# A 16-block fp32 transformer step: elementwise pairs of the norms moved to GpSimd, one demodulation kept in its PSUM bank, block 0's key demodulation by one-hot products, and new instruction orders

## The chip, the cores and the metric

One core of a Trainium2 chip. The core has TensorE (PE) for matmuls, VectorE (DVE), ScalarE (ACT) and GpSimd (POOL) for elementwise work, and SyncE (SP), which issues most transfers; each takes its instructions in the order of its own queue. The metric is the device time of one execution in microseconds, the median over the runs.

## The reference

A batch of 128 sequences of 64 tokens with 256 features, `x` (8192 tokens in all), goes through four residual layers, each conditioned on vectors of the sequence:

```python
x = x + L0(x, cond_512)   # kx = demodulated linear of x * style_k; softmax(kx kx^T / 4) kx, 16 heads of 16;
                          # then a demodulated linear with style_o
x = x + L1(x, cond_512)   # relu(x @ w_down[b]) @ w_up[b] + x, weights made per sequence
x = x + L2(x, ids, ...)   # h = ln(ln(x) * pw_g[id] + pw_b[id]) ...; t, s: ln(x) with table gains;
                          # m, n, r: x plus a vector of the sequence;
                          # silu([h t m n r s] @ W1 + b1) @ W2 + b2, then ln
x = x + L3(x, cond_512)   # out = x @ (U[b] V) + bias[b], U from cond_512 @ W_dec, rank 30
```

`demodulated` means that output column o of sequence b is multiplied by rsqrt(sum_i (w[o,i] * style[b,i])^2 + 1e-8). Everything is fp32 apart from one-hot tables in bf16.

## The kernel before

The tokens are cut into NBLK = 16 blocks of T = 512 tokens (NB = 8 sequences); a block has NTILE = 4 tiles of 128 tokens. `attention(blk)` makes layer 0 of a block, `rest(blk, ...)` layers 1 to 3. A prologue (`prologue_keys`, `prologue_rest`) makes styles, demodulations, tables, the sequence vectors, and the decoder factors U of all sequences.

Layouts alternate: features on partitions (`xT`, `x1T`, `x2T`, `xnT`, `hnT`, `g`; 128 x 2 x 512) for the wide matmuls, tokens on partitions (`x2`, `xn`, `h`, `x3`; four 128 x 256) for norms. TensorE's transposes lead from one to the other.

In a block: `xsT` = xT * style on GpSimd (L840). For each of the four tiles (`tile_attention`): keys (L930); `kxe` = bank * demodulation `dmk` on VectorE (L938); plus bias on GpSimd (L944); a 32 x 32 transpose on VectorE (L955); scores into the four banks `sc` (L986); their row maxima `mt` on VectorE (L995, two of 128x1024 per tile); the maxima are transposed (L1005, L1011, L1018, L1025) and subtracted by one-hot products (L1036); exp on ScalarE (L1050); the weighted sum (L1060); normalization (L1072 to L1079); a transpose (L1090) and the output style (L1095). Then the output linear (L896), for each half of the features:

```python
y = bank * demod_o                  # L903, VectorE, PSUM -> SBUF slot "tmp"
x1T = y + ob + xT                   # L914, VectorE
```

Layer 1 is L1118 (down), L1127 (relu), L1136 (up) and the sum x2T = 2 * x1T + up (L1149, VectorE, two halves). Layer 2 transposes x2T (L1190), copies it (L1193), takes statistics (L408, L409 on VectorE), r = (var + eps)^-0.5 on GpSimd (`rstd`, L413 and L415), the offset nr = -mean * r on VectorE (`offset`, L1168), and normalizes on ScalarE (`normalize`, L1176). `h` = xn * gain (L1201, VectorE) + shift (L1208, GpSimd), with gain and shift gathered per token (`pw`, L855), is normalized again. `xnT` and `hnT` come by transposes (L1226) and copies (L1229), are multiplied by gains made with one-hot products (L1235, L1244), and go into the first linear (L1259, 16 matmuls of 512 columns with L1268). L1274 and L1277 make the silu, L1290 the second linear, L1295 its bias; the third norm follows, then x3 = normalized * lg (L1301, VectorE) + x2 (L1304, GpSimd). Layer 3 transposes x3 (L1316, L1321), multiplies by U of the block (`uT`, L1333), adds a bias (L1344), multiplies by V (L1359), adds x3 (L1367) and stores (L1371).

For `dmk` the prologue writes the demodulations of all sequences to DRAM (`demod_k`, L505), and every block reads its eight rows back, each repeated over 64 partitions (two transfers, L797). U goes to DRAM through `uu` (128 x 4096): for each of the two halves of the features 30 products (L750), the bias (L755), and four transfers to `ud` (L769); both halves use the same `uu`.

The order of the work is not that of the program text. `Plan` records every operation with its engine, an assumed duration, what it reads and writes and the buffer slots it needs, then walks through an assumed execution and, on each engine, takes among the operations that could start first the one with the lowest turn. The turns are tables of numbers, `TURNS`: one for the prologue, one for the first block, one for all middle blocks, one for the last. `KEEP` favours a matmul of the tiling mode that TensorE is in; `pair=True` marks a VectorE operation that in the plan shuts GpSimd out; `load` gives a transfer's assumed time. Slots are handed out in the same walk, and some pass to heirs (`HEIRS_*`) once the prologue is done with them.

Of the kernel before, what the change touches and what calls it, by code (L numbers as in the profile page):

```python
# [9 lines left out]
F32 = mybir.dt.float32  # L10
# [3 lines left out]
ALU = mybir.AluOpType  # L14
AX = mybir.AxisListType

B, S, F = 128, 64, 256
NT = B * S
C = 2
T = 512  # L20
NB = T // S
NBLK = NT // T
NTILE = T // 128
H, D = 16, 16
K3 = 30
K3P = 32
# [6 lines left out]
SLOTS_FT = (("xT", 2), ("xsT", 1), ("osT", 1), ("x1T", 2), ("x2T", 2), ("hnT", 1), ("xnT", 1), ("g", 1), ("s2", 1))  # L33
SLOTS_1 = (("att", 2), ("p1", 8))
SLOTS_2 = (("kT", 2), ("kR", 2), ("v", 1), ("ao", 2), ("tmp", 3), ("pw", 3), ("p2", 8))
SLOTS_U = 16

HEIRS_1 = ("x3", "x2", "h", "xn", "x3", "x2", "h", "x3")
HEIRS_U = ("x2", "x2", "x2", "x2", "xn", "xn", "xn", "xn", "h", "h", "h", "h", "x3", "x3", "x3", "x3")
HEIRS_2 = ("pw", "v", "kT", "kR", "pw", "tmp", "ao", "v")  # L40
# [17 lines left out]
class Plan:  # L58
# [10 lines left out]
    SWITCH, KEEP = 0.08, 30.0  # L69
# [7 lines left out]
    def op(self, eng, took, emit, reads=(), writes=(), busy=None, claims=(), full=0.0, mode=0, pair=False):  # L77
# [3 lines left out]
        o = dict(eng=eng, took=took, busy=took if busy is None else busy, emit=emit, full=full, mode=mode, pair=pair)  # L81
# [34 lines left out]
    def order(self):  # L116
# [18 lines left out]
        at, self.cells, landed, mode, locked = {}, {}, [], 0, 0.0  # L135
        ready = [o for o in ops if not o["wait"]]
        done = []
        while ready:
            best = {}
            for o in ready:  # L140
                pe = o["eng"] == "PE"
                other = at.get("POOL", 0.0) if o["pair"] else locked if o["eng"] == "POOL" else 0.0
                t = max([other, at.get(o["eng"], 0.0)] + [ops[d]["end"] + lag for d in o["deps"]])
# [8 lines left out]
                if t is not None:  # L152
                    turn = o["prio"] - (self.KEEP if pe and o["mode"] == mode else 0.0)
                    best.setdefault(o["eng"], []).append((t, turn, o["n"]))
# [16 lines left out]
            o["start"], o["end"] = t, t + busy + (o["took"] - o["busy"])  # L171
# [26 lines left out]
    -8200 -7966 -18394 1443 -1847 8122 14127 3541 20535 -16013 -17005 17606 -23774 5435 -34510 18558 2614 3537 -253  # L198
    20624 27103 -438 -1494 25293 9034 -42362 -12205 -43231 28467 -41057 -40764 10345 1927 -10856 23480 5587 -11535
    -2699 -12811 11563 -1709 -22299 -17435 24238 -9733 103 2193 12913 3946 2640 -12255 -6755 -6353 2747 30512 7567  # L200
    -13172 -40570 9903 5897 -16559 -43835 2104 4978 -9021 8382 5714 28619 2514 -41088 -38702 21169 -15013 -4235 -6370
    -36126 27882 -7087 5065 6270 7617 -15738 -41818 -24576 -46135 -5769 -179 25293 -47598 501 -36248 -39392 -5815
    -17772 -6386 -44534 12570 -44284 -21576 -10573 -19779 6641 3353 -10423 -12878 -41598 -36305 18779 -11277 5632
# [1291 lines left out]
```

## Time and profile before

| | |
|---|---|
| median of 3 runs (lowest, highest) | 927.48 us (926.0, 928.22) |
| the profiled execution: time, span | 929.13 us, 927.4 us |
| mean granted TensorE clock | 0.972 |
| busy: TensorE, VectorE, GpSimd, ScalarE | 826.4, 698.2, 509.8, 446.5 us |
| HBM read, written | 75.94 MB, 13.24 MB |

The span reaches from the first to the last instruction; the time has a little around it. A row of a group of instructions gives line, engine, operation, what it writes and reads, how many, busy time and mean duration, and then the engine's idle time before them with what ended it. A wait reads "engine line <- engine line": who waited for whom. A window gives each engine's busy time in a stretch, and in parentheses how many instructions. Neighbouring instructions of one engine overlap by some hundredths of a microsecond in the records.

### The profile page before, as it was taken

The numbers are of one execution on the slowest core, as the hardware profiler recorded it, in microseconds if no ns is written. First come the engines' busy times: TensorE is split into PE (matmuls) and PEld (weight loads), VectorE is DVE, ScalarE is ACT, GpSimd is POOL, SyncE is SP. The second block draws the span as 40 slices with busy tenths as digits, with TensorE's granted clock in tenths as the row PEclk, the third lists the DMA queues.
The fourth block names the chain that finished last, engine by engine and source line by source line (L and its number), as shares of the span: only waits on it lengthen the run. The fifth ranks groups of instructions, "written<-read, shape, count | busy, mean of one in ns | idle before, by whom it ended". The sixth has DMA issues, their size and how long they took to land.

```text
span 927.4 us, 23950 instructions
## 1 busy us (share of the span) xinstructions
PE 826.4 (89%) x9744; PEld 535.9 (58%) x9744; DVE 698.2 (75%) x1539; ACT 446.5 (48%) x821; POOL 509.8 (55%) x602
## 2 busy tenths in 40 slices
PE   3686889898999999998989999999989899899893
PEld 2465646556565656666565656566665656465542
DVE  3595976969696987969696969879696969686643
ACT  1452444537364554545373645545453736444331
POOL 4371771837557482838475573829384755724221
PEclk9697999999999999999999999999999999999896
DMA  8866641232415132332324152322323231202000
GB/s 258 226 175 212 198 131 56 82 101 82 124 47 149 56 115 69 98 93 82 112 82 124 47 149 56 108 74 92 101 80 113 76 98 48 80 3 58 12 24 24
DMA packets 63103, 90.75 MB, mean 98 GB/s; under 512 B 6352, under 2 KB 46736, under 8 KB 62992
## 3 DMA queue, kind: packets, MB, share of 16 engines
q1 hardware_dynamic: 57872, 72.43, 26.9%
q0 software_dynamic: 5120, 16.78, 6.3%
q8 instruction: 77, 1.26, 0.6%
q14 instruction: 34, 0.28, 0.1%
HBM read 75.94 MB, written 13.24 MB: 96 GB/s over the span
## 4 chain that ended last, share of the span: by engine, by line
PE 71%; DVE 17%; DMA 3%; ACT 3%; issue 2%; POOL 1%; SPq 0%; another core or an unknown queue 0%; DVEq 0%; POOLq 0%; ACTq 0%
PE bank L1259 24%; PE sc L986 7%; PE bank L1060 7%; PE bank L1290 6%; PE bank L896 6%; DVE mt L995 5%; PE bank L930 4%; PE bank L973 3%; DVE x2T L1149 2%; PE bank L1190 2%; PE bank L1118 2%; PE bank L1226 2%; PE sc L1036 1%; PE bank L1090 1%; DVE st L408 1%
## 5 line engine op out<-in xcount | busy, mean ns | idle before, releaser
L995 DVE TENSOR_REDUCE mt<-sc 128x8 f32<-128x1024 f32 x128 | 154.6, 1211 | 11.8 <-PE sc L986 8.2
L1050 ACT ACTIVATE e<-sc 128x1024 f32<-128x1024 f32 x128 | 126.5, 1030 | 64.7 <-PE sc L1036 56.4
L1005 ACT COPY mt<-mt 128x16 f32<-128x16 f32 x64 | 13.0, 203 | 165.0 <-DVE mt L995 164.8
L1079 POOL TENSOR_TENSOR att<-ao,rz 128x256 f32<-128x256 f32 x44 | 27.2, 623 | 100.0 <-DVE rz L1076 92.5
L930 PE MATMUL bank<-wk,xsT 128*128 128x256 f32 x256 | 68.4, 402 | 0.4 <-ACT p L976 0.4
L1244 DVE TENSOR_TENSOR hnT<-hnT,bank 128x512 f32<-128x512 f32 x32 | 21.9, 688 | 59.8 <-PE bank L1235 39.2
L1259 PE MATMUL bank<-g,w_t 128*128 128x512 f32 x128 | 63.2, 617 | 4.1 <-DVE g L1244 4.1
L1259 PE MATMUL bank<-hnT,w_h 128*128 128x512 f32 x128 | 63.9, 605 | 1.4 <-DVE hnT L1244 1.4
L1259 PE MATMUL bank<-xnT,w_s 128*128 128x512 f32 x128 | 65.1, 593 | 0.0
L1290 PE MATMUL bank<-w,s 128*128 128x256 f32 x256 | 62.5, 386 | 0.7 <-DVE s L1277 0.7
L896 PE MATMUL bank<-osT,wo 128*128 128x512 f32 x128 | 60.9, 602 | 0.6 <-DVE osT L1095 0.6
L1259 PE MATMUL bank<-x2T,w_x 128*128 128x512 f32 x128 | 60.8, 595 | 0.0
L413 POOL TENSOR_SCALAR ry<-mvy 128x4 f32<-128x4 f32 (+1 forms) x19 | 9.2, 482 | 91.9 <-DVE mvy L409 91.7
L944 POOL TENSOR_TENSOR kxe<-kxe,kbr 128x256 f32<-128x256 f32 x64 | 46.8, 732 | 22.5 <-DVE kxe L938 18.0
L986 PEld LDWEIGHTS sc<-kR,kT 24*128 24x128 f32 x1408 | 44.1, 189 | 24.0 <-issue 12.5
L986 PE MATMUL sc<-kR,kT 24*128 24x128 f32 x1408 | 52.5, 286 | 3.4 <-ACT e L1050 3.4
L930 PEld LDWEIGHTS bank<-wk,xsT 128*128 128x128 f32 x256 | 47.6, 201 | 9.9 <-issue 3.7
L1290 PEld LDWEIGHTS bank<-w,s 128*128 128x128 f32 x256 | 46.0, 190 | 9.1 <-DVE s L1277 2.2
L408 DVE BATCH_NORM_STATS2 st<-uu 128x6 f32<-128x256 f32 x118 | 47.4, 409 | 2.1 <-ACT uu L1193 1.4
L870 POOL TENSOR_TENSOR wdn<-gdb,late 128x512 f32<-128x512 f32 x32 | 40.8, 1277 | 10.0 <-PE bank L1118 5.3
L855 POOL DMA_INDIRECT pw<-in_pw,idx x39 | 38.7, 993 | 11.5 <-issue 8.9
L1060 PE MATMUL bank<-e,p 128*32 128x128 f32 x1280 | 44.9, 276 | 0.0
(193 smaller groups left out, 2064.1 us busy)
## 6 DMA issues: line engine op xcount, KB each, us to landing
xT<-in_xT SPq DMA_DIRECT2D x32, 256.0 KB
dmk<-demod_k SPq DMA_DIRECT2D x32, 256.0 KB
gdb<-dgdb SPq DMA_DIRECT2D x16, 512.0 KB
ubb<-ugub SPq DMA_DIRECT2D x32, 256.0 KB
wup<-ugub SPq DMA_DIRECT2D x32, 256.0 KB
out_x<-uu SPq DMA_DIRECT2D x37, 128.0 KB
ud<-uu SPq DMA_DIRECT2D x8, 512.0 KB
uT<-ud SPq DMA_DIRECT2D x16, 256.0 KB
```

The lines of the kernel that those rows point to most:

```text
L408: dve(256, lambda: nc.vector.bn_stats(st.t, x.t), [x], [st])
L855: lambda tl=tl, n=n: nc.gpsimd.indirect_dma_start(out=pw[tl].t, out_offset=None, in_=a["pw"], in_offset=bass.IndirectOffsetOnAxis(ap=idx[: ...
L870: lambda w=w, dp=dp: nc.gpsimd.tensor_tensor(w(), gdb.t[:, :, 0:64], dp, ALU.mult),
L896: nc.tensor.matmul(ps.t, owT[:, c, bass.ts(oc, 128)], osT.t[:, c, :], start=(c == 0), stop=(c == C - 1))
L930: nc.tensor.matmul(ps.t[:, :F], xsT.t[:, c, bass.ts(tl, 128)], kwT[:, c, :], start=(c == 0), stop=(c == C - 1))
L944: lambda: nc.gpsimd.tensor_tensor(kxe.t[:, :, 0:D], kxe.t[:, :, 0:D], heads(kinds["kbr"][0]), ALU.add),
L986: nc.tensor.matmul(sc.t[:, q, bass.ts(g, 128)], of_g(kT.t)[r, g, :], of_g(kR.t)[r, g, :], start=(g == 0), stop=(g == 3))
L995: lambda two=two: nc.vector.tensor_reduce(mt.t[:, two, 0:4], sc.t[:, two, :].rearrange("p q (g n) -> p q g n", g=4), AX.X, ALU.max),
L1050: lambda k=k: nc.scalar.activation(es[k].t, sc.t[:, 2 * k : 2 * k + 2, :], AF.Exp, scale=0.25),
L1060: nc.tensor.matmul(ps_o.t[32 * q : 32 * q + 32, bass.ts(g, 128)], v.t.rearrange("p (g q d) -> p g q d", g=4, q=4)[:, g, q, :], es[q // 2]. ...
L1259: lambda ps=ps, w=w, src=src, fc=fc, c=c, n=n: nc.tensor.matmul(ps.t, w.t[:, c, bass.ts(fc, 128)], src.t[:, c, :], start=(n == 0 and c == ...
L1290: nc.tensor.matmul(ps.t[:, :F], s2.t[:, c, bass.ts(tl, 128)], w2.t[:, c, :], start=(c == 0), stop=(c == C - 1))
```

## The change

- `offset`: nr = -mean * r in two GpSimd operations (the mean times -1, then times r) in place of one on VectorE, for the three norms of a block.
- h = xn * gain and x3 = normalized * lg: the multiplications move from VectorE to GpSimd, ahead of the sums that were there.
- x1T: the product with `demod_o` is written back to the PSUM bank it came from, not to a `tmp` slot; the second operation reads the bank.
- Block 0's `dmk` is made in the prologue: for each tile a product of a one-hot matrix (8 sequences x 512 tokens, a new input `seqs`) with the first eight rows of the demodulations, and a ScalarE copy. Block 0's two transfers fall away.
- U's second half gets its own `uu` (a twin); when the prologue is done with it its memory serves as `hnT`, `xnT`, `g` and `s2`, which have no slots of their own any more.
- `Plan`: transfers share one assumed queue of bytes, `KEEP` is 20 and distinguishes only tiled from untiled matmuls, and the walk has slightly different rules. No operation is marked `pair`. There are new tables for the second block and the last but one, and all numbers in the tables are new, so that the instructions on every engine, SP's transfers included, stand in another order. In that order `early` is SP's eighth transfer (it was the third).

```diff
...
-SLOTS_FT = (("xT", 2), ("xsT", 1), ("osT", 1), ("x1T", 2), ("x2T", 2), ("hnT", 1), ("xnT", 1), ("g", 1), ("s2", 1))
+SLOTS_FT = (("xT", 2), ("xsT", 1), ("osT", 1), ("x1T", 2), ("x2T", 2))
...
-SLOTS_U = 16
+SLOTS_U = 16, 4
...
+HEIRS_V = ("hnT", "xnT", "g", "s2")
...
-    SWITCH, KEEP = 0.08, 30.0
+    SWITCH, KEEP = 0.08, 20.0
...
-                    turn = o["prio"] - (self.KEEP if pe and o["mode"] == mode else 0.0)
+                    turn = o["prio"] - (self.KEEP if pe and bool(o["mode"]) == bool(mode) else 0.0)
...
-    uu = slots.tile([128, B * K3P], F32, name="uu", tag="uu")
-    kinds["uu"] = [uu[:, bass.ts(n, F)] for n in range(SLOTS_U)]
+    uus = [slots.tile([128, B * K3P], F32, name=f"uu{c}", tag=f"uu{c}") for c in range(C)]
+    for name, t, n in zip(("uu", "uv"), uus, SLOTS_U):
+        kinds[name] = [t[:, bass.ts(i, B * K3P // n)] for i in range(n)]
...
-        name = "prologue" if blk < 0 else "first" if blk == 0 else "last" if blk == nblk - 1 else "middle"
+        ends = {-1: "prologue", 0: "first", 1: "second", nblk - 2: "last but one", nblk - 1: "last"}
+        name = ends.get(blk, "middle")
...
+        seqs0 = Buf("p2")
+        load(NB, 2048, lambda: nc.sync.dma_start(out=seqs0.t[:NB, :], in_=a["seqs"]), [], [seqs0])
+        dmk0 = Buf("dmk")
+        for tl in range(NTILE):
+            ps = Buf("bank")
+            product(
+                0.43,
+                ps,
+                128,
+                slice(0, F),
+                lambda tl=tl: [(seqs0.t[:NB, bass.ts(tl, 128)], dk.t[:NB, :])],
+                [dk, seqs0],
+                [dmk0],
+            )
+            act(F, lambda ps=ps, tl=tl: nc.scalar.copy(dmk0.t[:, tl, :], ps.t[:, :F]), [ps], [(dmk0, tl)])
...
-        for half in range(2):
+        if not blk:
+            dmk = dmk0
+            plan.noted[blk] += 2
+        for half in range(2) if blk else ():
...
-            ps, y = Buf("bank"), Buf("tmp")
+            ps = Buf("bank")
...
-                lambda ps=ps, y=y, oc=oc: nc.vector.tensor_tensor(
-                    y.t.rearrange("p (b t) -> p b t", t=S),
+                lambda ps=ps, oc=oc: nc.vector.tensor_tensor(
+                    ps.t.rearrange("p (b t) -> p b t", t=S),
...
-                lambda y=y, oc=oc: nc.vector.scalar_tensor_tensor(
-                    x1T.t[:, oc, :], y.t, ob[:, oc : oc + 1], xT.t[:, oc, :], ALU.add, ALU.add
+                lambda ps=ps, oc=oc: nc.vector.scalar_tensor_tensor(
+                    x1T.t[:, oc, :], ps.t, ob[:, oc : oc + 1], xT.t[:, oc, :], ALU.add, ALU.add
...
-            dve(
-                4,
-                lambda: nc.vector.scalar_tensor_tensor(nr.t, mv.t[:, :, 0], -1.0, r.t, ALU.mult, ALU.mult),
-                [mv, r],
-                [nr],
-            )
+            pool(0.24, lambda: nc.gpsimd.tensor_scalar(nr.t, mv.t[:, :, 0], -1.0, None, ALU.mult), [mv], [nr])
+            pool(0.24, lambda: nc.gpsimd.tensor_tensor(nr.t, nr.t, r.t, ALU.mult), [nr, r], [nr])
...
-            dve(
-                256,
-                lambda tl=tl: nc.vector.tensor_tensor(h[tl].t, xn[tl].t, pw[tl].t[:, 0:F], ALU.mult),
+            pool(
+                0.65,
+                lambda tl=tl: nc.gpsimd.tensor_tensor(h[tl].t, xn[tl].t, pw[tl].t[:, 0:F], ALU.mult),
...
-            dve(256, lambda tl=tl: nc.vector.tensor_tensor(x3[tl].t, x3[tl].t, lg, ALU.mult), [x3[tl]], [x3[tl]], pair=True)
+            pool(0.65, lambda tl=tl: nc.gpsimd.tensor_tensor(x3[tl].t, x3[tl].t, lg, ALU.mult), [x3[tl]], [x3[tl]])
...
+    a["seqs"] = np.repeat(np.eye(NB, dtype=f32), S, axis=1)
```

## The prediction

> **What bounds the kernel now.** I read the page's totals first, then the chain that ended last, which repeats every 51.1 us: the two x2T operations (L1149) start at 267.01, 318.10, 369.18 us. From block 1's at 163.68 to block 14's at 830.80 lie 13 such periods, 667.1 us; before them stands a start of 163.7 us, behind them an end of 96.6 us. Then one period cut where its chain changes hands.
>
> ```profile
> span 927.4 us, 23950 instructions
> PE 826.4 (89%) x9744; PEld 535.9 (58%) x9744; DVE 698.2 (75%) x1539; ACT 446.5 (48%) x821; POOL 509.8 (55%) x602
> ```
>
> ```profile
> core 0: us, PE busy (x) PEld busy (x) DVE busy (x) ACT busy (x) POOL busy (x), PEclk, DMA share, GB/s
> 318.10:333.15 15.05, 12.47 (x184) 9.15 (x184) 14.66 (x38) 10.41 (x22) 13.40 (x15) 1.00 0.29 88
> 333.15:359.15 26.00, 26.00 (x217) 15.40 (x218) 17.07 (x33) 9.36 (x17) 14.47 (x18) 1.00 0.39 110
> 359.15:369.18 10.03, 9.87 (x198) 6.54 (x195) 9.29 (x23) 7.10 (x13) 3.27 (x5) 1.00 0.19 55
> sum 51.08, PE 48.33 PEld 31.09 DVE 41.02 ACT 26.87 POOL 31.14; mean PE 16.11 PEld 10.36 DVE 13.67 ACT 8.96 POOL 10.38
> ```
>
> The middle stretch (the first layer, L1259) is TensorE's alone: 26.00 of 26.00. In the other two VectorE is busy 23.95 of 25.08 us while TensorE loses time. So 75% for VectorE is an average over a stage where it has room and two where it is full. The waits of TensorE in this period:
>
> ```profile
> PE bank L1190 <- DVE x2T L1149: 0.9, 1, 0.9
> PE bank L1359 <- DVE zT L1344: 0.8, 1, 0.8
> PE bank L1011 <- DVE uu L1367: 0.6, 1, 0.6
> PE bank L1011 <- ACT mt L1005: 0.3, 1, 0.3
> PE bank L1259 <- DVE g L1244: 0.2, 1, 0.2
> ```
>
> Nearly all end on VectorE. They sum to 2.8, the same as 51.08 - 48.33 = 2.75 us of idle TensorE: the most that a period can give while its matmuls stay as they are.
>
> **Part 1: norms and h to GpSimd (16 blocks).** The moved rows, and the GpSimd row nearest to their successors (minimum/median/maximum ns):
>
> ```profile
> L1168 DVE SCALAR_TENSOR_TENSOR nr<-mv,r x16: 161/760/772, 117.0 to 882.6; 128x4 f32<-128x4 f32 x16
> L1168 DVE SCALAR_TENSOR_TENSOR nrh<-mvh,rh x16: 161/578/580, 135.4 to 893.5; 128x4 f32<-128x4 f32 x16
> L1168 DVE SCALAR_TENSOR_TENSOR nry<-mvy,ry x16: 151/153/162, 159.7 to 911.2; 128x4 f32<-128x4 f32 x16
> L1201 DVE TENSOR_TENSOR uu<-uu,p x17: 409/414/760, 126.2 to 890.1; 128x256 f32<-128x256 f32 x17
> L1208 POOL TENSOR_TENSOR p<-p,pw x14: 712/730/996, 119.3 to 884.9; 128x256 f32<-128x256 f32 x14
> ```
>
> VectorE loses, by this period's rows, three offsets (0.76 + 0.58 + 0.15 = 1.49 us), four L1201 (2 x 0.58 + 2 x 0.41 = 1.98) and four L1301 (2 x 0.58 + 2 x 0.42 = 2.00): 5.5 us of 41.0 (less where rows overlap by some 0.07). In the full stretches stand of these, by the timeline, the first offset (0.68 in the chain), L1201 twice (0.74) and L1301 once (0.75) in the first, and L1301 three times (about 1.18) in the third: 3.35 us. That is more than the 2.75 that TensorE idles, so VectorE stops being what decides there.
>
> GpSimd keeps its eight sums (L1208, L1304) and gets eight multiplications of 128x256 at 0.73 = 5.8 and six small operations, which I put at the row of L413 (128x4 with a constant, 0.23), 1.4 in all; a two-input 128x4 has no row but the power (1.04), which bounds it from above (three per block, 2.4 more at most); I take 0.23 as the simple one is nearer. 31.1 + 7.2 = 38.3 us of a period of 49: 78%, still below TensorE.
>
> Here a rule speaks against the change. The Trainium skill, "GPSIMD Engine Reference", Engine selection, sends elementwise work to VectorE because GpSimd is about twice as slow with two inputs. The rows give 730/414 = 1.76 for one operation. By the rule (2 x 0.41 = 0.83) GpSimd has 39.1 us, by the row 38.3; both fit, and the rule counts the engine's time, not which engine is full. What is queued behind it is the danger: the products and sums for h and for x3 are now one queue, 8 operations instead of 4, so each set ends about 8 x 0.70 - (0.45 + 4 x 0.73) = 2.2 us later, and with them the transposes of L1226 and L1316. A second page works for the change: "SBUF — State Buffer", Who interferes with whom, says that a VectorE operation with two SBUF inputs and a GpSimd operation that reads SBUF exclude each other. The row that bears on it is L1168: 0.76 and 0.58 for four elements where GpSimd works, 0.15 where it idles. With a lock the three offsets are worth 1.49 per block, without 0.46; I take the row. No large VectorE operation of the changed kernel reads two SBUF tensors, so the 0.75 to 1.0 tails of L1201 and L1208 should go too.
>
> The first norm's path: in the chain the offset ends 3.7 us after the statistics (L413 at 323.56, then a 1.27 us L883 in between, L415, a VectorE maximum, offset ended at 327.29). In the new queue stand only L413's successor, one offset product, the power, one kxe sum and the other offset product: 0.23 + 0.23 + 1.04 + 0.73 + 0.23 = 2.5 us. So 1.2 earlier.
>
> **Part 2: x1T in its bank.** L903 (0.69) keeps its length if a result into PSUM costs what one into SBUF does; no row has it; between -0.05 and +0.15 each. L914 (0.75) becomes a PSUM and an SBUF input: L1149's form, 0.68. Two of each per block: from -0.25 to +0.2, taken -0.1; a bank is held 0.7 us longer, which is in the range.
>
> **Part 3: new orders.** TensorE's matmuls in a block are the same. Between L1136 and the transposes that wait for x2T (0.9 us idle now, one small transpose between) the new order puts a transpose, the 16 shifts and two transposes, 0.11 + 0.34 + 0.22 by the chain, 0.56 more than before. So of 2.75 idle I expect 2.2 back: 0.34 of the 0.9 and some 0.2 elsewhere stay. **13 x 2.2 = 28.6 us.** Bounds: 0 if GpSimd is late, 2.75 + 1.5 (TensorE rows are stretched where it runs dry: 32 L1060 take 1.19 there and 1.01 elsewhere), that is 0 to 55.
>
> **Part 4: the start.** Block 0's demodulation now goes through DRAM:
>
> ```profile
> 19.00 2.64 SPq L797 DMA_DIRECT2D dmk<-demod_k  x4
> 29.46 0.76 DVE L938 TENSOR_TENSOR kxe<-bank,dmk 128x256 f32<-128x256 f32 x2 [3.71 <-DMA dmk<-demod_k]
> ```
>
> The reciprocal it needs ends at 12.8. In its place: four K=8 products on TensorE (0.67 each at the low clock, by L423's 128x256) and four copies on ScalarE (0.37). But `early`, third in SP's queue, is now eighth: 5 x 0.47 = 2.3 us of issue, up to 3 with the bytes. ScalarE also loads its table four times, not two: 2 x 1.28. The four products stand in TensorE's queue behind L713's successor, which needs `late`; that landed at 14.0 and is again issued near 6.4, with the 16 KB of `seqs` next after it, so neither is later than the reciprocal. First kxe near 12.8 + 3 + 0.7 + 0.4 = 17, 12.5 us earlier. Removed from the queue of SP: two transfers of 0.61 issue, one added. Further, uu gets a twin, so the second decoder half no longer waits until the first is written: TensorE's longest wait of the start (L1060 behind a VectorE sum that waits for ud, 6.5 us) goes. Against full credit (19): the DMA engines are 91% busy to 29.5 us and 67% from there to 112, VectorE 64 of those 82.5 us, ScalarE pays 2.6. Bounds 0 and 19; I take **8**, nearer to the low end as the same bytes must still come.
>
> **Part 5: the end.** No other block hides the last x3. Four L1301/L1304 pairs ran from 912.05 to 916.33; eight GpSimd operations at 0.68 apart need 5.4: +1.2; two offsets +0.3 each, less what fewer VectorE operations give: **+1.2**.
>
> Sum: 927.4 - 28.6 - 8 + 1.2 = 892.0 span. The profiled execution took 929.13, 1.73 more than its span; the median of the runs, 927.48, is 1.65 less than that. 892.0 + 1.73 - 1.65 = **892**.
>
> **Rivals.**
> A, above: 880 to 905, whose own range is period gains of 1.5 to 2.75 and starts of 3 to 13. For it: the two full VectorE stretches. Chance 0.63.
> B, more: rows of stretched TensorE shrink as well and the start gives 15: 13 x 3 + 15 - 1 = 53, 874 (866 to 880). Chance 0.08.
> C, GpSimd's queue takes over half: h and x3 come 2.2 us later and 1.2 of it shows per period, so 1.0 is left: 927.5 - 13 - 5 + 1.2 = 911 (905 to 925). For it: 13.40 of 15.05 us busy in the first stretch, and L1304's result was TensorE's 5.0 us wait at the end. Against: in the middle stretch 11.5 us of it are free. Chance 0.22.
> D, nothing: VectorE's freed time falls beside TensorE's full stretch and the start stays DMA-bound; 927. Chance 0.02.
> E, slower: L1316, in TensorE's queue ahead of the keys of the next block (L930), waits for the eight-operation x3 queue, every period. It decides from (28.6 + 8 - 1.2)/13 = 2.7 us per period on; at 3.2 us the time is 934. Against: the orders can put other matmuls ahead of L1316. Chance 0.05.
>
> About 0.2% is what a measurement of this kernel can tell from no change. Faster 0.63 + 0.08 + 0.22 = 0.93, same 0.02, slower 0.05. The range leaves out the lower half of B, 917 to 925 of C, D and E (0.04 + 0.09 + 0.07): 873 to 917.
>
> **What would show it.** A period of 48.9 between x2T's; TensorE's waits on L1149's and L1344's successors below 1 us together; VectorE near 35.5, GpSimd near 38 per period; no GpSimd wait for VectorE at h; kxe first at 17 us; block 1's x2T near 156; the last x3 about 5.4 us after its first norm. Wrong: long waits of TensorE for the x3 or h of GpSimd, of the first-layer product for the norm, or a first kxe at 17 with block 1's x2T still near 163.

## The result, and the profile after

| | before | after | forecast |
|---|---|---|---|
| median beside each other, 15 runs each (lowest, highest) | 928.3 (925.13, 938.46) us | 917.98 (914.46, 925.62) us | 892 (873 to 917) |
| ratio, 95% interval | | 0.9879 [0.9846, 0.9911] | 0.962 |
| profiled execution: time, span | 929.13, 927.4 us | 915.64, 913.9 us | span 892.0 |
| start, to block 1's x2T | 163.60 | 164.04 | -8 |
| 13 periods, to block 14's x2T | 667.12 | 649.27 | -28.6 |
| end | 96.63 | 100.56 | +1.2 |

The kernel is 1.2% faster; 3.8% was forecast, and the median lies 1 us above the range. The three stretches of the two profiled executions differ by +0.4, -17.9 and +3.9 us, together the 13.5 of the span. The forecast was -35.4, so 8.4 us are missing at the start, 10.7 in the middle and 2.7 at the end.

The totals of the page, after (busy time, share of the span, instructions of each engine):

```profile
span 913.9 us, 23971 instructions
PE 835.8 (91%) x9752; PEld 538.6 (59%) x9752; DVE 635.7 (70%) x1363; ACT 452.0 (49%) x827; POOL 608.3 (67%) x826
```

One period of the changed kernel, cut where its chain changes hands, as it was cut for the kernel before:

```profile
core 0: us, PE busy (x) PEld busy (x) DVE busy (x) ACT busy (x) POOL busy (x), PEclk, DMA share, GB/s
416.70:431.75 15.05, 13.92 (x175) 10.03 (x175) 12.70 (x31) 9.13 (x18) 14.73 (x22) 1.00 0.30 90
431.75:456.34 24.59, 24.32 (x232) 14.39 (x230) 14.84 (x30) 11.65 (x20) 16.38 (x19) 1.00 0.38 116
456.34:466.37 10.03, 10.03 (x195) 6.68 (x193) 9.47 (x21) 6.27 (x11) 6.19 (x11) 1.00 0.18 56
sum 49.67, PE 48.27 PEld 31.10 DVE 37.01 ACT 27.05 POOL 37.29; mean PE 16.09 PEld 10.37 DVE 12.34 ACT 9.02 POOL 12.43
```

VectorE has gone from 41.0 to 37.0 us of a period, GpSimd from 31.1 to 37.3. TensorE has the same work (48.27, before 48.33) and idles 1.40 us instead of 2.75. TensorE's waits in this period, after:

```profile
PE sc L1096 <- DVE mTb L1085: 0.8, 1, 0.8
PE bank L1290 <- DVE mTb L1085: 0.3, 1, 0.3
PE bank L1150 <- ACT uu L1284: 0.2, 1, 0.2
```

The waits for x2T, zT and uu are gone. A new one has come: the 16 shifts, the one-hot products that subtract the maxima (L1096, before L1036), wait for mTb (L1085), the transposed maxima that they multiply, and all that stands behind them waits too. The moved rows, after (count, then minimum, median and maximum ns), and the two of x1T:

```profile
L1226 POOL TENSOR_SCALAR nr<-mv x16: 225/226/245, 116.6 to 863.2; 128x4 f32<-128x4 f32 x16
L1227 POOL TENSOR_TENSOR nr<-nr,r x16: 198/202/377, 121.3 to 864.5; 128x4 f32<-128x4 f32 x16
L1257 POOL TENSOR_TENSOR uu<-uu,p x18: 717/729/744, 130.4 to 868.2; 128x256 f32<-128x256 f32 x18
...
L964 DVE TENSOR_TENSOR bank<-bank,demod_o x32: 670/699/700, 92.3 to 854.4; 128x512 f32<-128x512 f32 x32
L975 DVE SCALAR_TENSOR_TENSOR x1T<-bank,early,xT x32: 726/751/752, 93.2 to 855.2; 128x512 f32<-128x512 f32 x32
```

The start, cut at the first x2T of block 0 and of block 1, before:

```profile
0.00:110.34 110.34, 75.34 (x819) 58.42 (x820) 72.37 (x133) 37.05 (x73) 51.22 (x66) 0.88 0.74 217
110.34:163.60 53.26, 47.64 (x552) 29.18 (x550) 39.67 (x88) 26.84 (x48) 27.65 (x33) 1.00 0.37 98
```

and after:

```profile
0.00:100.67 100.67, 72.85 (x699) 52.48 (x703) 61.19 (x115) 38.95 (x74) 48.08 (x61) 0.83 0.63 183
100.67:164.04 63.37, 59.03 (x685) 39.64 (x678) 47.85 (x96) 26.59 (x48) 34.49 (x46) 1.00 0.52 161
```

Block 0's x2T comes 9.7 us earlier, and block 1's does not: work that stood ahead of the first now stands ahead of the second, where TensorE is busy 59 of 63 us. The column behind GpSimd's, the granted clock, is lower in the first part.

The changed kernel, run again beside later experiments, took 911.6 us, 2.1% less than the kernel before beside it (`c_after`, below). Its time differs by 0.7% between the two occasions, so kernels are compared with those run together with them, in the groups of the tables. Starts, periods, ends and waits are of one profiled execution of each kernel.

### The profile page after: what moved, and what is told of

The parts are those of the page before. It is cut to its first block, busy times and chain, and to the rows that moved or that the text cites. A ratio compares the mean times of both kernels' runs of the same rounds, so it can differ in the third digit from the quotient of the medians.

```text
span 913.9 us, 23971 instructions
## 1 busy us (share of the span) xinstructions
PE 835.8 (91%) x9752; PEld 538.6 (59%) x9752; DVE 635.7 (70%) x1363; ACT 452.0 (49%) x827; POOL 608.3 (67%) x826
## 4 chain that ended last, share of the span: by engine, by line
PE 71%; DVE 9%; ACT 6%; POOL 3%; issue 2%; POOLq 0%; ACTq 0%; DVEq 0%
PE bank L1314 22%; PE sc L1046 7%; PE bank L1120 6%; PE bank L957 6%; PE bank L1345 5%; PE bank L990 5%; DVE mt L1055 3%; PE bank L1033 3%; PE sc L1096 2%; PE bank L1150 2%; PE bank L1290 2%; ACT uu L1284 2%; PE bank L1178 2%; PE bank L1196 2%; PE bank L1371 2%
## 5 line engine op out<-in xcount | busy, mean ns | idle before, releaser
L1055 DVE TENSOR_REDUCE mt<-sc 128x8 f32<-128x1024 f32 x128 | 151.7, 1205 | 18.5 <-PE sc L1046 18.4
L1299 DVE TENSOR_TENSOR uu<-uu,bank 128x512 f32<-128x512 f32 x96 | 63.9, 680 | 13.9 <-PE bank L1290 13.0
L990 PE MATMUL bank<-wk,xsT 128*128 128x256 f32 x256 | 68.4, 400 | 0.7 <-POOL xsT L900 0.7
L1314 PE MATMUL bank<-uu,w_t 128*128 128x512 f32 x128 | 66.4, 627 | 2.1 <-DVE uu L1299 1.4
L1314 PE MATMUL bank<-uu,w_s 128*128 128x512 f32 x128 | 67.2, 607 | 0.0
L1314 PE MATMUL bank<-x2T,w_x 128*128 128x512 f32 x128 | 64.5, 605 | 0.0
L453 POOL TENSOR_SCALAR ry<-mvy 128x4 f32<-128x4 f32 (+1 forms) x19 | 4.4, 232 | 88.1 <-DVE mvy L449 87.9
L1345 PE MATMUL bank<-w,uu 128*128 128x256 f32 x256 | 61.7, 384 | 1.0 <-DVE uu L1332 1.0
L1046 PE MATMUL sc<-kR,kT 24*128 24x128 f32 x1440 | 58.0, 291 | 2.6 <-ACT e L1110 2.6
L1314 PE MATMUL bank<-uu,w_h 128*128 128x512 f32 x128 | 59.0, 595 | 0.1
L1046 PEld LDWEIGHTS sc<-kR,kT 24*128 24x128 f32 x1440 | 49.2, 193 | 16.3 <-issue 5.7
L990 PEld LDWEIGHTS bank<-wk,xsT 128*128 128x128 f32 x256 | 47.7, 198 | 17.2 <-issue 10.3
L1345 PEld LDWEIGHTS bank<-w,uu 128*128 128x128 f32 x256 | 46.2, 190 | 8.6 <-DVE uu L1332 1.6
L1132 DVE STREAM_TRANSPOSE ao<-bank 128x512 f32<-128x512 f32 x45 | 32.1, 713 | 26.5 <-PE bank L1120 23.2
L915 POOL DMA_INDIRECT pw<-in_pw,idx x39 | 40.1, 1028 | 7.8 <-issue 7.0
```

The costliest lines, as they stand in the source:

```text
L990: nc.tensor.matmul(ps.t[:, :F], xsT.t[:, c, bass.ts(tl, 128)], kwT[:, c, :], start=(c == 0), stop=(c == C - 1))
L1046: nc.tensor.matmul(sc.t[:, q, bass.ts(g, 128)], of_g(kT.t)[r, g, :], of_g(kR.t)[r, g, :], start=(g == 0), stop=(g == 3))
L1055: lambda two=two: nc.vector.tensor_reduce(mt.t[:, two, 0:4], sc.t[:, two, :].rearrange("p q (g n) -> p q g n", g=4), AX.X, ALU.max),
L1299: lambda ps=ps, src=src, dst=dst, c=c: nc.vector.tensor_tensor(dst.t[:, c, :], src.t[:, c, :], ps.t, ALU.mult),
L1314: lambda ps=ps, w=w, src=src, fc=fc, c=c, n=n: nc.tensor.matmul(ps.t, w.t[:, c, bass.ts(fc, 128)], src.t[:, c, :], start=(n == 0 and c == ...
L1345: nc.tensor.matmul(ps.t[:, :F], s2.t[:, c, bass.ts(tl, 128)], w2.t[:, c, :], start=(c == 0), stop=(c == C - 1))
```

## The experiments

"Periods" are the 13 from block 1's to block 14's x2T.

### The moves and the orders, apart

Engines and orders were crossed. `e1`: the kernel before, order unchanged, with the multiplications and offsets on GpSimd. `e2`: the changed kernel's order with both on VectorE. `e3`: only the offsets on VectorE.

```diff
 # e1, at L1168, L1201, L1301 of before
-nc.vector.scalar_tensor_tensor(nr.t, mv.t[:, :, 0], -1.0, r.t, ALU.mult, ALU.mult)
+nc.gpsimd.tensor_scalar(nr.t, mv.t[:, :, 0], -1.0, None, ALU.mult); nc.gpsimd.tensor_tensor(nr.t, nr.t, r.t, ALU.mult)
-nc.vector.tensor_tensor(h[tl].t, ...)    # x3 likewise
+nc.gpsimd.tensor_tensor(h[tl].t, ...)
 # e2, at L1226, L1227, L1257, L1356 of after; e3: the first two only
-nc.gpsimd ...
+nc.vector ...      # same places in the order; the offset one operation again
```

> The kernel before with only the moves of part 1: the multiplications of h and x3 and the three offsets are issued on GpSimd, every operation in the place where the old order has it. Theory M (the moves carry the period, the new orders hardly matter): the period falls from 51.08 to near 49.7 as in the changed kernel, 13 x 1.4 = 18 less, 1.2 more at the end: near 910. Theory O (an order has to be made for the moved work): in the old order TensorE's last wait stays the x2T wait of 0.9 us, only part of VectorE's 3.35 us counts, 0.3 to 0.6 a period: 919 to 924. Theory Q (GpSimd's queue): eight operations in a place made for four push the x3 and h transposes back by up to 2.2 us a period: 928 to 950.

> The changed kernel with part 1 taken back: the eight multiplications a block and the offsets (as one operation each) are issued on VectorE, at the places of the new order. Theory M: VectorE has 5.5 us more a period, the gain of the period is lost, 917.98 + 18 = 936 or more. Theory O: the new order alone holds the period at 49.7 to 50.2, 916 to 925, and the end is about 2 us shorter as no eight-operation queue stands there.

> The changed kernel with the offsets alone back on VectorE, one operation each. If the lock between the two engines is what made them dear (0.76 and 0.58 for four elements), the first norm of each block is 0.3 to 0.7 later and VectorE loses 0.5 to 1.5 a period: 921 to 930. If GpSimd's two small operations (0.23 and 0.20) cost as much on the path as one of VectorE: 917 to 919.

| run together | median us | ratio, 95% | start | periods | end |
|---|---|---|---|---|---|
| e1 | 958.68 | 1.0301 [1.0224, 1.0379] | 162.59 | 697.84 | 97.1 |
| e2 | 984.83 | 1.0597 [1.0516, 1.0678] | 166.6 | 716.78 | 100.1 |
| e3 | 942.16 | 1.0119 [1.0039, 1.0198] | 170.05 | 672.86 | 100.6 |
| e4 (middle of the changed kernel) | 919.01 | 0.9896 [0.9821, 0.9972] | 162.11 | 652.12 | 98.4 |

Neither half of the change is worth anything alone. The moves in the old order cost 28 us (31 in the periods) although VectorE has only 36.7 us per period there; the new order with the old engines costs 55. Not all of that is waiting: in the periods of e1 12.9 us, and in those of e2 21.6 us, are TensorE's work at half clock, of which before and after have none. No run has an order made afresh for the old engines, so what a better order would give without the moves is open. e1's GpSimd around a first norm (start, duration, operation):

```profile
491.49 0.23 POOL L413 TENSOR_SCALAR r<-mv 128x4 f32<-128x4 f32 x1
491.69 1.27 POOL L883 TENSOR_TENSOR wup<-wup,late 128x512 f32<-128x512 f32 x1
492.92 1.04 POOL L415 TENSOR_TENSOR r<-r,mhalf 128x4 f32<-128x4 f32 x1
493.93 1.27 POOL L884 TENSOR_TENSOR wup<-wup,ubb 128x512 f32<-128x512 f32 x1
495.27 0.24 POOL L1169 TENSOR_SCALAR nr<-mv 128x4 f32<-128x4 f32 x1
495.60 0.20 POOL L1170 TENSOR_TENSOR nr<-nr,r 128x4 f32<-128x4 f32 x1
```

Two `wup` operations of 1.27 us stand ahead of four-element ones, and the offset ends 4.3 us after r began; in the changed kernel 2.4. e1's period is 52.87 us and TensorE idles 4.1 of them, with these two waits among others:

```profile
PE bank L1011 <- ACT mt L1005: 1.2, 1, 1.2
PE bank L1193 <- DVE x2T L1149: 1.2, 1, 1.2
```

GpSimd does not lack time there (busy 37.4 of 52.9 us); what the timeline shows is who stands ahead in its queue. How much of the 31 us that makes is not shown. Against e3, e2's periods are longer by 43.9, so the eight multiplications alone are worth 3.4 us per period in the new order; against e4, e3's by 20.7, so the offsets are worth 1.6, the less certain of the two, as e4's unaltered middle varied between 49.4 and 51.2. Both are more than the busy time that returns to VectorE, most likely because the order was laid out for the other engine. The offsets themselves are short in e3 and e2. How long one takes depends on what GpSimd does beside it; before, in e3 and in e2, the offset and the GpSimd operation nearest to it:

```profile
479.24 1.27 POOL L884 TENSOR_TENSOR wup<-wup,ubb 128x512 f32<-128x512 f32 x1
479.78 0.76 DVE L1168 SCALAR_TENSOR_TENSOR nr<-mv,r 128x4 f32<-128x4 f32 x1
...
490.85 1.27 POOL L937 TENSOR_TENSOR wdn<-wdn,gdb 128x512 f32<-128x512 f32 x1
491.83 0.30 DVE L1227 SCALAR_TENSOR_TENSOR nr<-mv,r 128x4 f32<-128x4 f32 x1
...
509.01 1.28 POOL L937 TENSOR_TENSOR wdn<-wdn,gdb 128x512 f32<-128x512 f32 x1
510.81 0.12 DVE L1227 SCALAR_TENSOR_TENSOR nr<-mv,r 128x4 f32<-128x4 f32 x1
```

Before and in e3 the offset ends within 0.03 us of the sum that GpSimd had begun earlier; in e2, whose multiplications are on VectorE, GpSimd's sum is over and the offset takes 0.12.

### The start

`e4` puts `early` and the style weights (L471), eighth and fourth in SP's queue, first; `e8` takes the one-hot products out and reads `dmk` of block 0 from DRAM again.

```diff
 # e4
+    done.insert(sp[0], done.pop(early_at))
+    done.insert(sp[0] + 1, done.pop(sp[3] + 1))
 # e8, at the four products and the copy L560
-        lambda tl=tl: [(seqs0.t[:NB, bass.ts(tl, 128)], dk.t[:NB, :])],
+        nc.sync.dma_start(out=dmk0.t[bass.ts(half, S), :, :], in_=src.to_broadcast([S, NTILE, F]))
```

> The changed kernel with the loads of early and of the key style's weights issued first and second instead of eighth and fourth; everything else in place. TensorE's first matmul, at 9.9 us, then comes at about 5.4. If the start is a chain that hangs on its head, the time falls by 3 to 4.5: 913.5 to 915. If the start is bound by what comes later (decoder loads in SP's queue, TensorE's work at half clock between 30 and 95 us), the time stays at 917 to 919 and only the first products are earlier.

> The changed kernel without the one-hot products: block 0's demodulation goes to DRAM and is read back by two transfers, all else in the new order. The first kxe then comes near 28 instead of 18.7. If the earlier attention of block 0 is worth the 8 us that the prediction gave it: 924 to 930. If the start is bound by the sum of its work, with TensorE at half clock wherever it is thin, the later attention is made up by block 1: 917 to 921.

TensorE's longest wait of the changed kernel is the one that e4 removes:

```profile
PE bank L463 <- DMA early<-in_early: 9.9, 1, 9.9
```

In e4 the first matmul starts at 3.6 instead of 9.9 us, but the second product waits for GpSimd's squares until 10.3 (12.5 in the changed kernel). Block 0's x2T comes 3.4 earlier, block 1's 1.9. The median, 919.01, shows no gain; but its interval is 14 us wide and no unaltered kernel ran beside it, so 2 us would not show. e8 lost: 919.53 where e5, e6 and e9, run beside it with the products (below), took 909 to 913. So by the medians the one-hot products help. The profiles show less of it: block 0's x2T came at 104.55, 3 to 5 us later than theirs, but block 1's at 169.5, and theirs at 165.3 to 169.5.

TensorE's time up to block 1's x2T, split into work at full clock, time lost to half clock (busy time times one minus the granted clock, over windows of 2 us) and idle. The record of the clock begins with its first change (at 18.1 us before, at 16.7 after), and the windows read the time ahead of it as full clock; but in after L990's products take 634 ns there, as in the recorded half clock behind it, and 379 at full clock, so that time is counted as half clock here:

| | work | lost | idle | sum |
|---|---|---|---|---|
| before | 111.6 | 11.4 | 40.6 | 163.6 |
| after | 114.6 | 17.3 | 32.1 | 164.0 |
| e8 (no one-hot products) | 113.3 | 13.7 | 42.5 | 169.5 |
| e9 (unaltered start, run beside e8) | 115.2 | 23.3 | 31.0 | 169.5 |

The idle time did fall by 8.5. The slower clock took 5.9 of it, and 3.0 more work (the four products, and other matmuls that the new order puts ahead of this x2T) took the rest. e8 and e9 show the same exchange: e9 idles 11.5 us less, and loses 9.6 more to the clock. To see whether the clock is a matter of density, `f1` and `f2` put additional matmuls ahead of the waiting ones in the prologue (f2 about twice as many), `s1` took 7 us of matmuls away (it leaves the decoder's second half of U out).

```diff
 # f1, f2: ahead of L1071, L1117, L1148 (f2 also L1031) where the plan has them between 18 and 92 us
+    nc.tensor.matmul(ps.t, ident, kwT.rearrange("p c n -> p (c n)"), start=True, stop=True)
 # s1, in the decoder, for c = 1
-    pe(0.22 * n + 0.05, by_k, [wd, early], [ps])
+    pe(0.22 * n + 0.05, (lambda: None) if c else by_k, [wd, early], [ps])
```

> The changed kernel with one idle product (128x512 into the bank that the next operation overwrites, 0.86 us at full clock) ahead of each of the 16 L1071, L1120 and L1150 that are planned between 18 and 92 us: 14 us more work for TensorE, put where it mostly waits. Theory H (the start is bound by TensorE, which loses 14 to 20 us to half clock there): the granted clock stays up, block 1's x2T comes 3 to 8 earlier, 909 to 914. Theory L (the start is bound by the chains of the attention and the decoder's transfers, the clock is a by-product): the products delay it, 919 to 928.

> As the run before it with more: two idle products ahead of L1071 and L1150, one ahead of L1120 and of L1033, 32 in all, 28 us of work at full clock. Theory H: the clock is at 1.0 from 25 us on, block 1's x2T comes 3 to 8 earlier unless the products themselves fill more than the idle time (about 46 us at full clock): 908 to 916. Theory L: 5 to 15 later, 923 to 933.

> The changed kernel once more, unaltered, as the measure for the runs beside it: 914 to 922, ratio to the kernel before near 0.988. Its profile tells how far the start (block 1's x2T at 164.0 in the first profile) and the period (49.4 to 50.4 there) move from one execution to another: the theory that the start is set by TensorE's half-clock stretches expects a start that moves together with the time TensorE loses to them (14.5 us up to block 1's x2T in the first profile, and about 20 with block 1's x2T at 169.5).

> The changed kernel with the decoder's second half left out: its 60 products (L807, 8 us of TensorE between 94 and 114 us) and its sums (L812) are not made and its half of uu is set to zero, so the last layer's result is wrong; its loads stay. Theory W (the start is one chain of work in which each us counts, so that what the earlier attention of block 0 won between 100 and 110 us went to the decoder that now stands there): block 1's x2T comes 8 to 14 us earlier than in the unaltered start beside it, 898 to 905. Theory D (transfers or the attention's own latency bind the start): 0 to 4 earlier, 908 to 913.

| | median us | ratio, 95% | block 0's x2T | busy to it, of that lost | between the x2T's |
|---|---|---|---|---|---|
| c_after (the changed kernel) | 911.6 | 0.979 [0.9757, 0.9824] | 100.89 | 73.6, 18.3 | 64.6 |
| f1 | 915.66 | 0.9839 [0.9804, 0.9874] | 103.85 | 78.6, 12.5 | 64.9 |
| f2 | 922.73 | 0.9913 [0.9883, 0.9943] | 109.88 | 88.6, 9.9 | 67.5 |
| s1 | 918.1 | 0.9879 [0.9828, 0.993] | 101.41 | 72.4, 17.9 | 65.3 |
| e9a (run beside s1, unaltered start) | 918.56 | 0.9869 [0.982, 0.9918] | 100.42 | 73.9, 19.2 | 69.9 |

Filling raises the clock, and costs more than the clock returns: f1 lost 5.8 us less and worked 11 more. Removing work did not pay in the median either (918.1 beside 918.56): in s1 the work between the two x2T's fell by 7 us (to 52.3), but the idle time there rose by 4 (to 8.3) and 4.7 were lost to the clock. Here is how the second part varies without any edit. After (granted clock in the column after GpSimd's):

```profile
120.00:125.00 5.00, 3.07 (x44) 2.25 (x42) 4.88 (x8) 3.26 (x6) 4.82 (x7) 1.00 0.71 270
125.00:130.00 5.00, 4.00 (x43) 2.24 (x47) 4.37 (x12) 3.49 (x6) 4.50 (x7) 1.00 0.88 219
130.00:135.00 5.00, 5.00 (x39) 2.65 (x36) 4.09 (x9) 0.65 (x3) 4.51 (x7) 1.00 0.90 246
```

and e9a, the same instructions in the same order up to there:

```profile
120.00:125.00 5.00, 3.36 (x54) 2.35 (x44) 4.97 (x9) 2.73 (x6) 4.82 (x7) 1.00 0.81 309
125.00:130.00 5.00, 4.16 (x29) 2.56 (x29) 2.76 (x8) 2.27 (x5) 4.53 (x7) 0.55 0.79 195
130.00:135.00 5.00, 4.54 (x36) 2.43 (x35) 2.52 (x4) 1.94 (x2) 4.51 (x7) 0.50 0.92 251
```

TensorE is thinly used at 120 to 125 in both; in one execution the clock halves afterwards and in the other it stays. Between the two x2T's the changed kernel needs 63.4 us where nothing is lost (after), 64.6 with 1.5 lost (c_after), 66.4 with 3.1 (e5), 68.1 with 4.9 (e9) and 69.9 with 6.3 (e9a): each us lost is about a us later, so with its full work this part is bound by TensorE. s1, where half of the 7 us taken away came back as idle time, shows that another bound lies only some 3 us below.

### The middle: what is left of the idle time

The filler waits for mTb. By the timeline of after (in brackets the idle time before, and who ended it):

```profile
416.58 0.33 PE L1071 MATMUL bank<-ident,mt 128*128 128x128 f32 x1
416.70 0.69 DVE L1209 SCALAR_TENSOR_TENSOR x2T<-x1T,bank 128x512 f32<-128x512 f32 x1 [0.16 <-PE bank L1196]
416.95 0.37 ACT L1078 ACTIVATE mX<-bank,early 128x128 bf16<-128x128 f32 x1 [0.66 <-PE bank L1071]
417.35 0.35 DVE L1085 SCALAR_TENSOR_TENSOR mTb<-bank,early,mX 128x128 bf16<-128x128 f32 x1
417.62 0.68 DVE L1209 SCALAR_TENSOR_TENSOR x2T<-x1T,bank 128x512 f32<-128x512 f32 x1
...
417.75 0.40 PE L1096 MATMUL sc<-mTb,sel 8*128 8x128 bf16 x16 [0.84 <-DVE mTb L1085]
418.09 0.44 PE L1150 MATMUL bank<-ident,att 128*128 128x128 f32 x2
418.36 1.12 PE L1246 MATMUL bank<-ident,x2T 128*128 128x128 f32 x8
```

mTb stands on VectorE between the two halves of x2T, but that is not what it waits for. Its maxima are transposed by L1071, TensorE's last matmul ahead of the shifts; ScalarE's mX follows within 0.05 us, mTb 0.03 us behind mX, and the shifts 0.05 us behind mTb. For this way round, 0.84 us from the end of one matmul to the start of the next, TensorE has nothing else. It is so from block 3 to block 14; before, it waited 0.9 us for x2T here. No run moved L1071 or put other work behind it. Two suspects for the rest were GpSimd's: in after, `nrh` (L1227) stands behind a `wdn` and a `kxe` sum (it starts 1.9 us after its power's end), and the two gathers of `pw` (L915) ahead of the attention product. `e5` moves the first up to its power, `e6` the gathers behind that product.

```diff
 # e5, for blocks 1 to 14
+        done.insert(rh[2] + 1, done.pop(rh[3]))
 # e6: the two L915 behind nrh go behind the next L1139
+            done.insert(to - 1, done.pop(n))
```

> The changed kernel; on GpSimd the product that makes the second norm's offset (nrh) stands directly behind its power, ahead of the wdn sum (1.27) and a kxe sum (0.72) that the new order puts between in blocks 1 to 14. ScalarE, idle 1.93 us for it in each period, then normalizes h about 1.9 earlier. Theory N (part of the missing 0.8 a period is that small product, late in GpSimd's longer queue: periods of 49.4 to 50.4 differ only there, and with the offsets on VectorE, 0.4 later, they were 51.0 to 51.9): the periods fall to 49.3 or less in every block, 0.3 to 1.0 a period, 905 to 914. Theory S (only the x2T gap bounds it): no change, 916 to 919, as the kxe sum and with it a transpose come 0.2 later.

> The changed kernel; in each middle block the two gathers that GpSimd issues behind nrh (1.08 and 0.95 us) go behind the next attention product. In that place VectorE's maximum waits 0.8 to 2.4 us after the scores' last product by the trace. If GpSimd's descriptor writing keeps VectorE from starting there, the maximum starts at once, the attention result comes some 2 us earlier, and the period falls by 0.3 to 0.8: 907 to 914. If the maximum waits for TensorE itself, nothing falls: 916 to 919.

| run together | median us | ratio, 95% | start | periods | end |
|---|---|---|---|---|---|
| e5 | 909.37 | 0.9774 [0.9742, 0.9806] | 167.09 | 644.47 | 100.3 |
| e6 | 912.78 | 0.9808 [0.9768, 0.9849] | 165.33 | 644.45 | 102.0 |
| e8 (middle unaltered) | 919.53 | 0.9895 [0.9854, 0.9936] | 169.52 | 644.82 | 98.3 |
| e9 (middle unaltered) | 909.61 | 0.9778 [0.9738, 0.9817] | 169.5 | 644.74 | 96.4 |

All four have a middle of 644.5 to 644.8, a period of 49.2, altered or not: neither suspect counted in these executions. The middle of the changed kernel itself takes 649.3 (after), 652.1 (e4), 649.5 (s1), 648.4 (e9a) in other executions, and 645.05 in c_after, where a period has only two waits, the same 0.8 for mTb and 0.2. `g2` was to show whether the gathers hold VectorE, by issuing each of the two twice.

> The changed kernel; in each middle block the two gathers behind nrh are issued twice (the second time with the same result), 2 us more on GpSimd, which is free behind them. Theory G (GpSimd's descriptor writing keeps VectorE from starting its maximum there, 0.4 to 2.4 us by the traces): the maximum waits about 2 longer and the period rises by 1 to 2: 925 to 940. Theory T (the maximum waits for the scores alone): nothing but the attention product comes later, which has 4 us of slack: the period is that of the runs beside it, 911 to 916.

It took 1010.78 us, 1.0877 [1.0822, 1.0933], and says nothing on that. g2's GpSimd:

```profile
487.98 0.95 POOL L915 DMA_INDIRECT pw<-in_pw,idx  x1 [4.58 <-DMA pw<-in_pw,idx]
```

The second gather into the same tile waits for the first one's landing, and the attention product behind them is late, for 64.7 us of TensorE's waiting (L1150) in all. That is a wait that the edit itself made.

### The end

In the last block no attention hides the x3 queue. `e9a` puts the multiplications of the last block back on VectorE (from that block's first layer on, the plan then also orders TensorE's matmuls differently); `e9` does so and lets its chains of first-layer matmuls begin with the x2T products, which need no gains.

```diff
 # e9a and e9
+            if last: dve(F, lambda: f(nc.vector), reads, writes)
+            else: pool(0.65, lambda: f(nc.gpsimd), reads, writes)
 # e9 alone
-            for n, (w, src) in enumerate(((w_t, gs), (w_x, x2T), (w_s, xnT), (w_h, hnT))):
+            for n, (w, src) in enumerate(terms if not last else (terms[1], terms[0], *terms[2:])):
```

> The changed kernel, the last block alone altered: its eight multiplications are on VectorE again, and its four products with x2T, which wait for nothing else, come before those with g (the order of a sum of products, nothing is left out). If the end's 100.6 us (96.7 before) come from GpSimd's queue of eight and from TensorE running dry and halved between 864 and 877: 3 to 6 less, 912 to 915. If the end is bound elsewhere: 917 to 919.

> The changed kernel with the last block's eight multiplications on VectorE again, and no more; the products with x2T stay in their place. If GpSimd's queue of eight is what made the end 3.9 longer than before: 100.3 falls to 96 to 98, and x3's last sum comes 4.9 after its first norm again. If the half clock between 867 and 877 made it: it stays at 99 to 101.

From the last block's x2T to the end: before 50.8 us, after 54.9, e9a 54.3, e9 50.8. e9a shortens the x3 chain (first norm to last sum: before 4.9, after 6.2, e9a and e9 4.5) and still gains next to nothing. What e9 adds is seen in TensorE's clock just behind h. After:

```profile
867.00:870.00 3.00, 2.67 (x8) 1.22 (x8) 1.54 (x5) 1.17 (x2) 3.00 (x5) 0.50 0.51 168
870.00:873.00 3.00, 2.00 (x3) 0.81 (x4) 2.83 (x9) 0.00 (x0) 1.30 (x4) 0.50 0.03 10
873.00:876.70 3.70, 3.70 (x7) 1.54 (x6) 0.75 (x2) 2.07 (x4) 1.32 (x3) 0.50 0.00 0
```

e9:

```profile
867.00:870.00 3.00, 2.68 (x13) 1.24 (x12) 2.72 (x8) 1.85 (x4) 3.00 (x4) 1.00 0.00 0
870.00:873.00 3.00, 1.89 (x8) 0.46 (x6) 2.73 (x9) 0.12 (x1) 1.93 (x5) 1.00 0.14 46
873.00:876.70 3.70, 3.52 (x18) 1.79 (x18) 1.80 (x4) 3.03 (x6) 0.00 (x0) 1.00 0.32 106
```

In after 7 matmuls fill the last window at half clock; in e9 the clock stays. e9's gain of 3.5 over e9a is more than executions differ by: the unaltered last block took 52.7 to 55.8 in ten profiles, and the four kernels below that have e9's took 51.3 to 51.4. In the medians it does not show: e9 is no faster than e5, which has the last block unaltered.

### Put together

`k1` is e5, e6 and e9; `k2` is k1 with e4; `k3` is k2 without e6, `k4` is k2 without e5.

> The changed kernel with three repairs together: the second norm's offset directly behind its power, the two gathers behind the attention product, and the last block with its multiplications on VectorE and the x2T products first. By the single runs: the end is 2 to 5 shorter, the periods 49.2 throughout: 905 to 910. If periods of 49.7 to 51 appear in the unaltered kernel beside it and not here, the gathers or the late offset make them; if they appear in both or in neither, they don't tell.

> The combination of the three repairs (offset behind its power, gathers behind the attention product, last block) with early and the key style's weights loaded first: 2 to 3 from the start, where the second product then waits for GpSimd's squares at 10.3, and 3 from the end: 905 to 909, the fastest so far. If the start makes up for nothing: 909 to 911.

> The combination with the gathers in their place again (offset behind its power, last block and early loads as in the combination). If the late offset was what let the period slip from 49.2 to 49.65: 49.2 throughout, about 907. If it was the gathers: 49.6 or more in an execution in which an unaltered middle has it, about 912; 49.2 in both runs of this call tells nothing.

> The combination with the second norm's offset in its late place again and the gathers behind the attention product. If the gathers let the period slip: 49.2 throughout, about 907. If the late offset did: 49.6 or more, about 912.

| | run beside | median us | ratio, 95% | start | periods | end |
|---|---|---|---|---|---|---|
| k1 | c_after | 909.59 | 0.9775 [0.974, 0.9809] | 167.22 | 644.15 | 97.5 |
| k2 | s1, e9a | 906.26 | 0.9758 [0.9718, 0.9798] | 168.77 | 644.24 | 97.6 |
| k3 | k4 | 914.17 | 0.9832 [0.9755, 0.9908] | 168.53 | 644.25 | 97.5 |
| k4 | k3 | 911.89 | 0.9793 [0.9724, 0.9862] | 169.55 | 644.44 | 97.7 |

k1 cannot be told from c_after beside it. k2 is the fastest measured: 2.4% below the kernel before, and below e9a, run beside it, by 12 us. Where e9a and s1 had periods of 49.65, k2 had 49.21; but k3 and k4, meant to show which of the two moves does that, both had 49.21 as well. That the moves steady the middle is therefore possible, not shown, and k2 is not separable from c_after, the changed kernel at its best.

## Why the prediction was right and wrong

**What bounds the kernel: right.** The idle time of TensorE in the middle did hang on VectorE: the waits for x2T and zT are gone, and what idles now is half of what did. Moving the work back lost it (e2).

**Part 1, sizes: mostly right.** An operation on GpSimd takes 0.729, as the row said; the offset pair 0.226 + 0.202, where 0.23 each was taken and up to 1.04 allowed. GpSimd has 37.3 us per period (38.3 forecast), the first norm's path 2.4 us (2.5). VectorE has 37.0, not 35.5: the removed rows were summed at full length, but rows lie over each other in the records, by 5.9 us in a period before and by 4.7 after. The exclusion of which the Trainium skill, "SBUF — State Buffer", Who interferes with whom, tells is what the offsets show: nr (0.76) ended with the GpSimd sum beside it and nrh (0.58) with the attention product, and beside no such operation they took 0.12 to 0.15. The lock also showed on the other side: in e9a and e9 GpSimd's sums of x3 took 0.90 to 1.00 beside VectorE's multiplications and 0.72 without. The rule of "GPSIMD Engine Reference" that speaks against the change did not decide: at the same prices the moves gave -64.7 us over the 13 periods in one order (after's 652.1 in e4 against e2's 716.8), +30.7 in the other.

**Part 2: 0 in place of -0.1.** L964 took 0.70, L903 had 0.69; L975 0.75, L914 0.75. A result into PSUM cost nothing that counts here, and an input from PSUM brought nothing. (The -0.1, 1.6 us over 16 blocks, had not been put into the sum either.)

**Part 3, the 2.2 per period: the step that failed is the filler.** The prediction said that a transpose, the 16 shifts and two transposes would cover 0.56 of x2T's 0.9, and counted the shifts as ready. They wait for mTb, and mTb, by way of ScalarE, for that same transpose: what was counted as filler is the first link of the filler's own inputs. So 0.8 of the 0.9 stayed under another name, with 0.2 to 0.3 elsewhere. That leaves 1.87 for a steady period (51.08 to 49.21), 24.3 for 13. In c_after 22.1 of it came, as the 13 are not all steady: the first became longer (52.3 before, 53.4 in after and c_after), the last gained most (52.9 to 49.2). The profiled execution after gave 17.9. The 4.2 between the two come and go between executions of the same middle: VectorE's maximum (L1055) began 0.1 to 0.4 us after its scores in most periods of 49.2, and 0.5 to 2.2 in most of the longer ones; why is open.

**Part 4, the -8: the gain came and was spent.** The first kxe came at 18.7 us (17 forecast, 29.5 before), the L1060 wait of 6.5 went, idle time fell 8.5. The step left out is TensorE's own time: it was costed as if waiting were all that block 1 depends on. Work went from ahead of block 0's x2T (63.9 us before, 55.6 after) to behind it, where TensorE is the bound, four products and other moved matmuls were added (3.0 in all), and 5.9 us more were lost to half clock ahead of the first x2T. The prediction's own sign of failure, "a first kxe at 17 with block 1's x2T still near 163", is what came. Why the clock fell more often is not shown; that idle time and lost clock trade against each other is (e8 and e9). `early`, eighth in the queue, was dreaded for 3 us, and the first matmul did come 4.5 later than before; what that costs at the end is not told apart by e4.

**Part 5, the +1.2: right for what it costed, and not all.** The x3 chain takes 6.2 instead of 4.9, +1.3. e1, the moves in the old order, agrees: its last block takes 51.8, 1.0 more than before. Another 2.6 came where nothing was costed, with the new order: in the last block TensorE worked 1.3 us longer (0.9 of it the clock) and idled 2.8 more, x3's chain included; the matmuls of L1314 wait 1.2 for a product with the gains (L1299), which stands behind h's statistics on VectorE. e9a shows that the multiplications alone are not it, e9 that the order of the first layer's products in the last block is, and its windows that the clock behind h is part of that.

**The rivals.** The time is C's (905 to 925), the cause is not. C had GpSimd's late h and x3 eat half the middle; TensorE's waits on either do not appear in a period, and C's "1.0 is left" was 1.4 to 1.9. E's wait of L1316's successor for x3 appears only at the end (8.8 us over the whole run). In e1, the old order, something of E's kind did come true: with the moves the kernel was 28 us slower, and the offsets behind `wup` are the part of GpSimd's queue that the timeline shows.

## What to carry to other kernels

Moving small operations to another engine is a change of two queues: look up what will stand ahead of each in the new one, and move and reorder together; here each alone cost 3 to 6% and both together gained 1.2 to 2.1. When a filler is to cover a wait, follow its own inputs back, engine by engine: here they led to TensorE itself. In a start or an end that idles much, account for TensorE's time as work, loss to the clock and idle: idle time that is removed can come back as a lower clock, or uncover a part that TensorE bounds.

## What the hardware did that was not expected

- The clock halved after stretches without a long gap. In e9a TensorE was busy 3.36 of the 5 us ahead of it and its longest single wait around there was 1.4 us; in after, with 3.07 of 5, it stayed full. The Trainium skill, "TensorE: Matmul & The Clock Gate", HAM oscillation, gives as its rule no idle gaps above some 3.4 us; by it nothing would be lost behind such a stretch, and e9a lost 6.3 us between the two x2T's. The section after it, A second HAM failure mode, tells of short but frequent idle times that do the same, without a size; this trace agrees with that, and here not in each execution.
- More matmuls in the prologue raised the clock (lost 18.3 to 12.5 and 9.9 us), and paid in neither run.
- A VectorE operation on four elements took 0.76 us where GpSimd was in a sum, to the end of that sum, and 0.12 where GpSimd was idle.
- The same kernel had periods of 49.2 us in some executions and 49.4 to 51.2 in others, at full clock.
